# A two-layer transformer on one core: pieces of the next projection issued in front of the turns of the softmax weights

## Chip, cores and metric

One core of a Trainium2 chip runs the whole program. The metric is device time in microseconds (us) from one launch: before the change the median of three runs is 591.26 us (590.09 to 594.53).

The engines are called by the profile's names: PE (matrix multiplies), PEld (the loading of their weights), DVE (vector engine), ACT (activation engine), POOL (GpSimd), SP (the queue that issues most DMAs). Each engine takes its own instructions in the order in which the program issues them; between engines only semaphores order the work.

## Reference

Two layers over x of 8 x 256 tokens x 128 channels. Each layer normalises x and adds an attention and a mixture of experts, both computed from the normalised x. Only layer 1 is touched here:

```python
# layer 1, xn = layernorm(x): 8 heads of queries, one head of keys and values, causal
q = (xn @ Wq + bq) + pe          # 8 heads x 128
k, v = split(xn @ Wkv + bkv);  k = k + pe
probs = softmax(mask(q @ k.T / sqrt(128)))
attn = (probs @ v) @ Wo
# 8 experts, each token takes the one of its largest gate
h = gelu(xn @ w1[e] + b1[e]);  ffn = (h @ w2[e] + b2[e]) * score
x = x + attn + ffn
```

## The kernel before

All arithmetic is in f32. The 2048 tokens are 16 tiles of 128, four blocks of 512 and eight batches of 256. Layer 0 fills the first 335 us of the span; layer 1 is one loop over the batches b = 0 to 7 (L1458 to L1493) and a short end for the last batch.

**A batch.** Its scores come in three parts u[0], u[1], u[2] of 128 query rows x 1024 columns: u[0] is the first 128 queries against 128 keys for all 8 heads, u[1] and u[2] the second 128 queries against 256 keys for four heads each. For each part:

- `l1_scores` (L1275): 8 multiplies (16 instructions for u[0], 4 heads and 8 instructions for the others) on PE into one of two large PSUM tiles;
- `l1_maxima` (L1289): DVE adds the causal mask (L1291) and takes row maxima (L1295);
- `l1_exp` (L1297): ACT takes one exponential per head (L1301), which frees the large PSUM tile;
- `l1_weigh` (L1309): DVE takes reciprocals of the sums (L1311), then POOL scales the weights (L1313; DVE does it for three parts of batches 6 and 7);
- `l1_turn` (L1321): DVE transposes the weights in 32 x 32 blocks (L1328), "the turn".

The product of weights and values (`l1_pv`, L1336, 72 multiplies) of batch b is issued in batch b+1 by `l1_previous` (L1446), after the scores of u[0] and u[1] of b+1; ACT copies its result out of PSUM (L1358). `l1_finish` (L1360) multiplies it with Wo and adds the result to the accumulator on DVE (L1373). PE issues the scores of u[2] after the product of values, since they need the PSUM tile of u[0].

**The projections of the next block.** Queries and keys of a block serve two batches. `l1_project` (L799) is a generator of 9 pieces for a block: the keys and eight heads of queries. A piece is one 128x512 multiply on PE (L807, two instructions) into one of three PSUM banks and one DVE instruction that adds bias and positions and writes SBUF (L814). Batches 0, 2 and 4 start a new block and issue 2 + 3 of its pieces, batches 1, 3 and 5 issue the other 2 + 2 (L1480 and L1489). Batches 6 and 7 have none left.

**Filling work.** `fill(b, k)` (L1416) issues what a table assigns to three places in the batch: in batches 0 to 2 the router (L1152, L364), in batches 3 to 5 the experts (`l1_experts`, L1242), in batches 5 to 7 the gathers of the experts' rows (`l1_back`, L1391). An expert tile is a multiply "up" (L1210, 8 instructions), a Gelu on ACT (L1219) and a multiply "down" (L1228, 8 instructions) with a DVE addition (L1237); every fourth tile needs four transposes on PE (L1200) and a copy on DVE (L1202). ACT loads another table when it goes from exponentials to Gelu and back. All of these, the pieces of the projections and `l1_finish` take turns on the same three PSUM banks ("bank", L105), so an instruction on PE may wait until DVE or ACT has read an earlier bank.

**The order around the change** is written out by hand (L1474 to L1493): on DVE the maxima of u[2], the turn of u[0], then the filling work of place 0, two pieces, and the reciprocals of u[1]; later the addition of `l1_finish`, the turn of u[1], two or three pieces, the turn of u[2], and the filling work of place 2.

Of the kernel before, what the change touches and what calls it, by code (L numbers as in the profile page):

```python
# [62 lines left out]
def two_layer_kernel(  # L63
# [48 lines left out]
    def seq(ins):  # L112

        return tc.keep_in_program_order(ins)
# [684 lines left out]
    def l1_project(blk):  # L799

        qT = work.tile([P, H1, BLK], F32, tag="qk", name=f"qT1_{blk}")
        kT = work.tile([P, BLK], F32, tag="kT1", name=f"kT1_{blk}")
        qk1[blk] = (qT, kT)
        for h in range(-1, H1):
            pos = (pe_s if h < 0 else peq_s).unsqueeze(1).to_broadcast([P, 2, S])
            ps = bank(f"qk1_{blk}_{h}")
            seq(nc.tensor.matmul(  # L807
                ps,
                lhsT=wk1_s if h < 0 else wq1_s[:, h, :],
                rhs=xT[:, ts(blk, BLK)],  # L810
                start=True,
                stop=True,
            ))
            seq(nc.vector.scalar_tensor_tensor(  # L814
                (kT if h < 0 else qT[:, h, :]).rearrange("p (b s) -> p b s", b=2),
                ps.rearrange("p (b s) -> p b s", b=2),
                bk1_s if h < 0 else bq1_s[:, h : h + 1],
                pos,
                ALU.add,
                ALU.add,  # L820
            ))
            yield

    project1 = l1_project(0)
# [299 lines left out]
    def l0_end(first, second):  # L1124

        l1_scores(first)
        l1_maxima(first)
        l0_drain(*last0)
        l1_scores(second)
        l0_finish(B - 1, l0_turn_back(*done))  # L1130
        norm1[NBLK - 1].moments()
        l1_maxima(second)
# [142 lines left out]
    def l1_scores(u):  # L1275
        qT, kT = qk1[u.b // 2]
        o = (u.b % 2) * S
        u.ps = big_tile(f"s_{u.name}")
        u.sc = u.ps.rearrange("p (h k) -> p h k", h=u.nh)
        for h in range(u.nh):  # L1280
            seq(nc.tensor.matmul(  # L1281
                u.sc[:, h, :],
                lhsT=qT[:, u.h0 + h, ds(o + u.t * P, P)],
                rhs=kT[:, ds(o, u.nk)],
                start=True,
                stop=True,
            ))

    def l1_maxima(u):  # L1289
        diag = u.sc[:, :, ds(u.t * P, P)]  # L1290
        seq(nc.vector.tensor_tensor(  # L1291
            diag, diag, mask.unsqueeze(1).to_broadcast([P, u.nh, P]), ALU.add
        ))
        u.m = small.tile([P, H1], F32, tag="m1", name=f"m1_{u.name}")
        seq(nc.vector.tensor_reduce(u.m[:, : u.nh], u.sc, AX.X, ALU.max, negate=True))  # L1295

    def l1_exp(u):  # L1297
        u.p = work.tile([P, u.nh, u.nk], F32, tag="e", name=f"p_{u.name}", bufs=4)
        u.sums = small.tile([P, H1], F32, tag="sums1", name=f"sums1_{u.name}")
        for h in range(u.nh):  # L1300
            seq(nc.scalar.activation(  # L1301
                u.p[:, h, :],
                u.sc[:, h, :],
                AF.Exp,
                bias=u.m[:, h : h + 1],
                accum_out=u.sums[:, h : h + 1],
            ))

    def l1_weigh(u):  # L1309
        rec = small.tile([P, H1], F32, tag="rec1", name=f"rec1_{u.name}")  # L1310
        seq(nc.vector.reciprocal(rec[:, : u.nh], u.sums[:, : u.nh]))  # L1311
        engine = nc.vector if (u.b, u.t, u.h0) in ON_VECTOR else nc.gpsimd
        seq(engine.tensor_tensor(  # L1313
            u.p, u.p, rec[:, : u.nh].unsqueeze(2).to_broadcast([P, u.nh, u.nk]), ALU.mult
        ))
# [5 lines left out]
    def l1_turn(u):  # L1321


        if u.h0 == 0:
            turned[u.b, u.t] = work.tile(
                [P, H1, u.nk], F32, tag="c" if u.t else "h", name=f"pT_{u.name}"
            )
        seq(nc.vector.transpose(  # L1328
            turned[u.b, u.t][:, ds(u.h0, u.nh), :].rearrange("p h k -> p (h k)"),
            u.p.rearrange("p h k -> p (h k)"),  # L1330
        ))
# [28 lines left out]
    def l1_finish(b, tt, oT):  # L1360
        ps = (bank if b + 1 < B else big_tile)(f"wo1_{b}_{tt[0]}")
        for t in tt:
            for h in range(H1):
                seq(nc.tensor.matmul(  # L1364
                    ps[:, ts(t, P)],
                    lhsT=oT[:, h, ts(t, P)],
                    rhs=wo1_s[:, h, :],
                    start=(h == 0),
                    stop=(h == H1 - 1),
                ))  # L1370
        n, c = 2 * b + tt[0], ds(tt[0] * P, len(tt) * P)
        a = acc[:, ds(n, len(tt)), :].rearrange("p t c -> p (t c)")
        seq(nc.vector.tensor_tensor(a, ps[:, c], a, ALU.add))  # L1373
        if b >= 6:
            nc.sync.dma_start(out_t[:, ds(n, len(tt)), :], acc[:, ds(n, len(tt)), :])
# [40 lines left out]
    def fill(b, k):  # L1416
        for f, args in between1.get((b, k), ()):
            f(*args)
# [27 lines left out]
    def l1_previous(b):  # L1446

        nonlocal oT
        if b > 0:
            po = l1_banks(b - 1)  # L1450
            for t in range(2):
                l1_pv(b - 1, t, po)
            if b + 1 < B:
                l1_spread(b + 1)
            oT = work.tile([P, H1, S], F32, tag="c", name=f"oT_{b - 1}")
            l1_out(slice(None), po, oT)

    for b in range(B):  # L1458
        u = [Part(b, k) for k in range(len(PARTS))]
        if b % 2 == 0 and b + 2 < B:  # L1460
            project1 = l1_project(b // 2 + 1)
        if b == 0:
            l0_end(u[0], u[1])
        else:
            l1_scores(u[0])
            l1_maxima(u[0])
            l1_scores(u[1])
            l1_maxima(u[1])
        l1_exp(u[0])
        l1_previous(b)  # L1470
        if b == 0:
            fill(b, 0)
        l1_weigh(u[0])
        l1_scores(u[2])  # L1474
        l1_maxima(u[2])
        l1_exp(u[1])
        l1_turn(u[0])
        if b > 0:
            fill(b, 0)
        for _ in range(2):  # L1480
            next(project1, None)
        l1_weigh(u[1])
        l1_exp(u[2])
        fill(b, 1)
        l1_weigh(u[2])
        if b > 0:
            l1_finish(b - 1, (0, 1), oT)
        l1_turn(u[1])
        for _ in range(3 - b % 2):  # L1489
            next(project1, None)  # L1490
        if b + 1 < B:
            l1_turn(u[2])
            fill(b, 2)  # L1493
# [100 lines left out]
```

## Time and profile before

| | |
|---|---|
| median of three runs | 591.26 us |
| the profiled execution's own time | 584.82 us |
| span of the profiled execution | 583.0 us |
| busy, share of the span | PE 85%, PEld 61%, DVE 62%, ACT 42%, POOL 35% |
| mean granted PE clock | 0.938 |
| the 24 turns, L1328 | 29.5 us, 1232 ns each; DVE idle ahead of them 7.1 us |
| 24 of the 27 pieces' DVE part in this loop (queries), L814 | 17.0 us, 733 ns each |

A batch begins here with the first mask addition on DVE (L1291 of u[0]), by the timeline:

| batch | 0 | 1 | 2 | 3 | 4 | 5 | 6 | 7 |
|---|---|---|---|---|---|---|---|---|
| start, us | 335.98 | 362.27 | 386.83 | 414.42 | 459.75 | 498.88 | 529.04 | 550.53 |

In a timeline a line is one or more instructions of a kind: start, duration, engine, line, operation, output and inputs, and in brackets how long the engine sat idle before and which instruction released it. In a table by windows the columns are the stretch, its length, busy time and number of instructions of PE, PEld, DVE, ACT and POOL, the granted PE clock as a share of full speed, the DMA share and GB/s.

### The profile page before, as it was taken

The page shows a single profiled execution, that of the slowest core. Times are in us where ns is not written, and L with a number is a line of the kernel's source. Part 1 is how long each engine was busy: PE and PEld are TensorE (multiplying, and loading weights), DVE is VectorE, ACT ScalarE, POOL GpSimd, SP SyncE. Part 2 cuts the span into 40 slices and gives each one's busy share as a digit, 9 for nine tenths or more (in the row PEclk, how much of TensorE's full clock was granted, in tenths as well). Part 3 has the DMA queues.
Part 4 walks back from the last instruction along what each step waited for, and adds up shares of the span by engine and source line. Part 5 has one row for each costly group of instructions (what it writes and reads, how often), then busy time and mean ns, then how long its engine had stood idle before and what let it go on. Part 6 is the DMA issues. An engine that isn't in the chain of part 4 may idle for free.

```text
span 583.0 us, 11267 instructions
## 1 busy us (share of the span) xinstructions
PE 497.3 (85%) x3996; PEld 354.1 (61%) x3996; DVE 359.4 (62%) x733; ACT 246.6 (42%) x681; POOL 205.6 (35%) x254
## 2 busy tenths in 40 slices
PE   4887688889998899967899968877969989989777
PEld 1633345656766577543554736666667878978666
DVE  5487954646756467637797467787633544527662
ACT  4616123434443254313443551523255584665161
POOL 6230023266432440274372032212576041124740
PEclk9999786989999799989999997996989999999977
DMA  3600411324443231011021130171048465512111
GB/s 108 189 1 19 133 33 44 110 72 121 126 128 105 74 77 38 28 46 29 17 69 45 37 92 19 37 200 41 25 108 234 145 149 180 158 55 64 33 32 56
DMA packets 61925, 47.78 MB, mean 82 GB/s; under 512 B 6389, under 2 KB 56781, under 8 KB 61869
## 3 DMA queue, kind: packets, MB, share of 16 engines
q1 hardware_dynamic: 57453, 38.59, 23.3%
q0 software_dynamic: 3840, 8.26, 5.9%
q8 instruction: 32, 0.52, 0.4%
q10 hardware_dynamic: 576, 0.20, 0.1%
q14 instruction: 24, 0.20, 0.1%
HBM read 38.78 MB, written 8.26 MB: 81 GB/s over the span
## 4 chain that ended last, share of the span: by engine, by line
PE 56%; DVE 20%; issue 9%; ACT 6%; POOL 4%; DMA 1%; SPq 0%; another core or an unknown queue 0%; POOLq 0%; ACTq 0%; DVEq 0%
PE s L894 7%; PE u L692 6%; PE pv L967 5%; PE s L1281 4%; PE d L709 4%; DVE mx L909 4%; PE u L1210 3%; PE o L1345 3%; PE d L1228 3%; PE qk L807 3%; PE s L940 3%; PE wo L1364 3%; ACT p L1301 2%; PE ds L760 2%; PE sh L745 2%
## 5 line engine op out<-in xcount | busy, mean ns | idle before, releaser
L952 ACT ACTIVATE eT<-s 128x1024 f32<-128x1024 f32 x64 | 65.5, 1024 | 138.9 <-PE s L940 95.7
L909 DVE TENSOR_REDUCE mx<-s 128x4 f32<-128x1024 f32 x64 | 77.7, 1220 | 32.0 <-PE s L940 14.3
L513 POOL DMA_INDIRECT xs<-xd,idx x62 | 63.0, 1016 | 67.0 <-issue 57.8
L894 PE MATMUL s<-qk 32*128 32x256 f32 x512 | 74.4, 422 | 13.6 <-DVE mx L909 8.8
L1313 POOL TENSOR_TENSOR p<-p,rec 128x1024 f32<-128x1024 f32 x21 | 39.8, 1896 | 112.3 <-DVE rec L1311 112.2
L1301 ACT ACTIVATE p<-s,m 128x256 f32<-128x256 f32 (+1 forms) x128 | 52.5, 443 | 62.5 <-DVE m L1295 51.0
L940 PE MATMUL s<-qa,qk 32*128 32x256 f32 x512 | 75.6, 414 | 2.5 <-DVE qa L921 2.3
L894 PEld LDWEIGHTS s<-qk 32*128 32x128 f32 x512 | 43.2, 195 | 41.7 <-DVE mx L909 17.9
L513 POOL DMA_INDIRECT yt<-yg,idx x48 | 48.9, 1020 | 47.1 <-issue 37.2
L1281 PE MATMUL s<-kT,qT 128*128 128x128 f32 (+1 forms) x256 | 49.8, 348 | 9.1 <-ACT p L1301 4.3
L940 PEld LDWEIGHTS s<-qa,qk 32*128 32x128 f32 x512 | 45.9, 192 | 10.6 <-DVE qa L921 5.0
L1345 PE MATMUL o<-pT,vrep 32*128 32x256 f32 x576 | 48.9, 407 | 3.9 <-DVE pT L1328 2.2
L1281 PEld LDWEIGHTS s<-kT,qT 128*128 128x128 f32 x256 | 40.0, 200 | 18.2 <-issue 6.9
L1345 PEld LDWEIGHTS o<-pT,vrep 32*128 32x128 f32 x576 | 40.5, 197 | 11.6 <-DVE pT L1328 2.4
L692 PE MATMUL u<-xg,gu_s 128*88 128x128 f32 x312 | 42.6, 278 | 1.6 <-issue 1.6
L967 PE MATMUL pv<-eT,va 128*32 128x256 f32 x512 | 39.3, 412 | 1.5 <-issue 1.4
L692 PEld LDWEIGHTS u<-xg,gu_s 128*88 128x88 f32 x312 | 37.1, 160 | 3.8 <-issue 3.8
L1219 ACT ACTIVATE h<-u,own_b 128x128 f32<-128x128 f32 x92 | 25.9, 375 | 27.7 <-PE u L1210 25.2
L1291 DVE TENSOR_TENSOR s<-s,mask 128x512 f32<-128x512 f32 (+1 forms) x24 | 20.9, 869 | 25.2 <-PE s L1281 21.5
L1364 PE MATMUL wo<-wo_s,oT 128*128 128x128 f32 x256 | 34.0, 297 | 2.1 <-DVE qT L814 1.8
L1364 PEld LDWEIGHTS wo<-wo_s,oT 128*128 128x128 f32 x256 | 33.0, 212 | 3.9 <-issue 3.3
L1328 DVE STREAM_TRANSPOSE pT<-p 128x1024 f32<-128x1024 f32 x24 | 29.5, 1232 | 7.1 <-POOL p L1313 7.1
(222 smaller groups left out, 843.2 us busy)
## 6 DMA issues: line engine op xcount, KB each, us to landing
w_up<-in_w_dram SPq DMA_DIRECT2D x30, 256.0 KB
gu_s<-in_gu_dram SPq DMA_DIRECT2D x39, 176.0 KB
vrep<-vd SPq DMA_DIRECT2D x32, 128.0 KB
w_down<-in_w_dram SPq DMA_DIRECT2D x16, 256.0 KB
yg<-ys SPq DMA_DIRECT2D x14, 256.0 KB
dn_s<-in_dn_dram SPq DMA_DIRECT2D x39, 88.0 KB
bias<-in_b_dram SPq DMA_DIRECT2D x23, 64.0 KB
acc<-in_x_dram SPq DMA_DIRECT2D x4, 256.0 KB
```

The source lines that it names most:

```text
L513: seq(nc.gpsimd.indirect_dma_start(out=dst, out_offset=None, in_=table, in_offset=bass.IndirectOffsetOnAxis(ap=idx[:, k : k + 1], axis=0), ...
L692: seq(nc.tensor.matmul(ps[:IC, ts(c, P)], lhsT=gu0_s[:, i % RING0, c, :], rhs=xg0.get(i), start=True, stop=True,))
L894: seq(nc.tensor.matmul(pv[:, jj, t, :], lhsT=qT[r : r + ROW, g, ds(o + t * P, P)], rhs=kT[r : r + ROW, g, ds(o, S)], start=True, stop=True,))
L909: seq(nc.vector.tensor_reduce(m[:, ds(2 * half, 2), :, D0 * ((g + 1) % NG)], pv, AX.X, ALU.max, negate=True))
L940: seq(nc.tensor.matmul(pv[:, jj, c, :], lhsT=kT[r : r + ROW, g, ds(o + c * P, P)], rhs=qa[r : r + ROW, g, :], start=True, stop=True,))
L952: seq(nc.scalar.activation(eT.rearrange("p j c q -> p (j c q)"), ps, AF.Exp, scale=SC0))
L967: seq(nc.tensor.matmul(po[ds(ROW * j, ROW), ts(g % 2, S)], lhsT=va_flat[:, ds(o, ROW)], rhs=eTs[j // 2][:, j % 2, c, :], start=(c == 0), s ...
L1281: seq(nc.tensor.matmul(u.sc[:, h, :], lhsT=qT[:, u.h0 + h, ds(o + u.t * P, P)], rhs=kT[:, ds(o, u.nk)], start=True, stop=True,))
L1301: seq(nc.scalar.activation(u.p[:, h, :], u.sc[:, h, :], AF.Exp, bias=u.m[:, h : h + 1], accum_out=u.sums[:, h : h + 1],))
L1313: seq(engine.tensor_tensor(u.p, u.p, rec[:, : u.nh].unsqueeze(2).to_broadcast([P, u.nh, u.nk]), ALU.mult))
L1345: seq(nc.tensor.matmul(po[n][:, ts(t, H1 * ROW)], lhsT=vrep[r : r + ROW, b % 2, j, :], rhs=pT[r : r + ROW, :, j, :], start=(j == 0), stop= ...
L1364: seq(nc.tensor.matmul(ps[:, ts(t, P)], lhsT=oT[:, h, ts(t, P)], rhs=wo1_s[:, h, :], start=(h == 0), stop=(h == H1 - 1),))
```

## The change

The change touches only the order of issue in the loop over batches. Up to batch 5 the two pieces come in front of the turn of u[0] instead of behind it, and the two or three later pieces come in front of the turn of u[1]. In batches 1 to 7 the filling work of place 0 also comes in front of the turn of u[0], and behind the two pieces. No instruction is added or removed. On PE the only new order is that in batches 1 to 5 two pieces precede the filling work of place 0; on ACT, POOL and SP every queue keeps its order.

```diff
@@ -1474,20 +1474,20 @@
         l1_scores(u[2])
         l1_maxima(u[2])
         l1_exp(u[1])
-        l1_turn(u[0])
+        for _ in range(2):
+            next(project1, None)
         if b > 0:
             fill(b, 0)
-        for _ in range(2):
-            next(project1, None)
+        l1_turn(u[0])
         l1_weigh(u[1])
         l1_exp(u[2])
         fill(b, 1)
         l1_weigh(u[2])
         if b > 0:
             l1_finish(b - 1, (0, 1), oT)
-        l1_turn(u[1])
         for _ in range(3 - b % 2):
             next(project1, None)
+        l1_turn(u[1])
         if b + 1 < B:
             l1_turn(u[2])
             fill(b, 2)
```

## Prediction

> **What bounds the kernel now.** I read the busy shares, the chain of work that ended last, what waits for the pieces' DVE part, then the timeline of each engine, batch by batch, and last the clock in stretches of 2 us. No engine bounds the loop throughout. Batches 0 to 2 are paced by DVE (router work, maxima, turns), batches 3 to 5 by PE and ACT in turn (experts), 6 and 7 by the softmax chain and the gathers. So each edit is worth only what its own batch lets through.
>
> Who waited for L814 from batch 0 on:
>
> ```profile
> who waited for it (us, times):
>   PE vg L784: 4.9, 1
>   PE wo L1364: 2.1, 2
>   PEld s L1281: 1.6, 2
>   PEld qk L807: 1.4, 1
>   PE s L1281: 1.3, 2
> ```
>
> A piece late on DVE holds a PSUM bank or a head of queries, so PE waits. The list adds up to some 11 us, but PE and its weight loads are counted side by side, and not all of it is on the path. The change lets these DVE parts run before a 1.2 us turn. The turns themselves can hardly gain (7.1 us of idle ahead of them, 2.95 of it in batch 0, the rest in batches 6 and 7, which have no pieces).
>
> DVE in batch 0:
>
> ```profile
> 349.31 1.25 DVE L1328 STREAM_TRANSPOSE pT<-p 128x1024 f32<-128x1024 f32 x1 [2.95 <-POOL p L1313]
> 350.48 0.71 DVE L814 SCALAR_TENSOR_TENSOR kT<-qk_-1_3850,bk_s,pe_s 128x512 f32<-128x512 f32 x1
> ```
>
> DVE is idle for 2.95 us, waiting for POOL, with a ready piece (PE was done with it at 344.4) behind the turn.
>
> DVE, PE in batch 3:
>
> ```profile
> 425.76 1.23 DVE L1328 STREAM_TRANSPOSE pT<-p 128x1024 f32<-128x1024 f32 x1
> 426.92 0.65 DVE L1202 COPY xgT<-xgT 128x512 f32<-128x512 f32 x1
> ```
> ```profile
> 423.69 0.60 PE L1200 MATMUL xgT<-ident,xs 128*128 128x128 f32 x4
> 427.68 2.72 PE L1210 MATMUL u<-xgT,w_up 128*128 128x128 f32 x15 [3.38 <-issue]
> ```
>
> PE stands still for 3.38 us, until DVE has done mask, maxima, turn and copy. What follows that gap is dear, as the windows show (clock in the third column from the end):
>
> ```profile
> 390.00:392.00 2.00, 0.00 (x0) 0.00 (x0) 1.18 (x1) 2.00 (x13) 0.00 (x0) 0.76 1.03 313
> 392.00:394.00 2.00, 1.61 (x4) 1.34 (x5) 0.20 (x1) 2.00 (x6) 1.29 (x1) 0.50 0.84 255
> ...
> 426.00:428.00 2.00, 0.33 (x3) 0.35 (x4) 1.57 (x2) 0.63 (x1) 1.69 (x3) 1.00 0.27 64
> 428.00:430.00 2.00, 2.00 (x15) 2.00 (x14) 0.00 (x0) 1.06 (x4) 1.42 (x3) 0.64 0.14 41
> 430.00:432.00 2.00, 2.00 (x11) 2.00 (x11) 0.00 (x0) 1.23 (x5) 1.70 (x2) 0.50 0.67 191
> ```
>
> After a gap the clock falls to half and stays there until a whole stretch of some 3.4 us is busy. From these fractions the falls lie at 350.1, 391.0, 401.3 and 428.6, the rises at 356.9, 397.8, 408.0 and 432.0: all whole multiples of 3.41 us apart.
>
> **The change, part by part** (times on the span of 583.0; a minus is earlier).
>
> *Batch 0, +0.1.* The two DVE parts go into the 2.95 us gap (2 x 0.7). The values' multiply (L784, at 351.33, idle 4.87 for this piece) then waits only for ACT's copy of the turned x, which ends at 350.2: 1.0 earlier. But its three following pieces run at half clock, 1.7 us each (PE 353.28 on), and now stand ahead of the turn of u[1]: DVE takes them at about 354.0, 355.9 and 356.8, then two turns (2.3), and ends at 359.8 instead of 359.7. Ends: -1.4 with the clock up, +1.1 if the multiply doesn't start earlier.
>
> *Batch 1, +1.2.* DVE is busy without a break from 369.86 to 391 and does the same work in another order: 0. The cover for the pieces is that PE finishes them (370.1 to 372) while DVE does the maxima. What is new is a gap: the product of values starts 1.1 earlier (it follows batch 0's last pieces and scores on PE), but the scores of u[2] still wait for ACT at 367.8. PE's idle 1.1 us there becomes 2.2. The nearest row is 390 to 392: after 2.4 us of product of values and 1.0 of idle within one 3.41 us stretch, the clock fell. Price: u[2]'s scores take 3.78 instead of 1.99 (both rows of L1281, at 392.39 and 367.83), +1.8, and the two pieces follow at half clock, together +2.7. Ends 0 and +2.7; I take +1.2, somewhat under half.
>
> *Batch 2, 0 for DVE, -1.0 for PE.* The order of DVE's 10 us changes, not the sum. At its end three pieces run 408.7 to 412.3; the third waits for the bank of the first, held by the turn (PE at 411.17, 1.4 us PEld wait). With the pieces first PE goes on at 410.1, and batch 3's scores come 1.1 earlier. The turns of u[1], u[2] end at 414.2 as before. Batch 3's product of values and u[2]'s scores run end to end on PE and keep 1.0.
>
> *Batch 3, -4.4 in all.* Place 0: u[2]'s maxima end at 424.7; two DVE parts (1.3) stand where one turn (1.16) stood, the copy is done at 426.7, and "up" starts at 426.8 instead of 427.68: -0.9. PE meanwhile does the two pieces (1.7), so the gap of 3.38 shrinks to about 1.8. A gap of 1.76 at 372.0 left the clock at 1.0. At full clock the 24 "up" take 2.7 instead of 4.55 and the first 8 "down" 0.9 instead of 1.7. Then the next four transposes must wait for rows that POOL gathers until 427.9 (landing about 430, estimated from the 2.06 us of an expert result's landing). The fourth tile's "up" starts about 431.4 instead of 435.15: -3.7. That two pieces (1.72) no longer stand at 437.04 brings nothing more: from there ACT paces (Gelu, table 1.28, four exponentials, table 1.28, Gelu of the next tiles at 442.17), and keeps -3.7. After `l1_finish` a piece no longer waits for the turn of u[1], and "down" at 453.19, idle 0.63 for that bank, starts 0.7 earlier. Sum -4.4. Ends: without the clock -1.6, with rows landing early -5.0.
>
> *Batch 4, -0.9.* The pieces leave 476.50 to 478.22 and fill a PE wait of 1.84 at 470.98 (for ACT's Gelu). ACT again paces after its table loads, until the Gelus at 481.57; from there the last "up" (483.27, behind a "down" idle 0.78) can come 0.9 earlier, and the output multiply with it. Ends -1.7 (all kept) and +0.15 (ACT keeps all).
>
> *Batch 5, 0.* The same move, into a wait of 1.39, but the batch ends on ACT: table, exponentials, table, Gelu at 519.81, "down" idle 0.93 for it. Ends -0.3, +0.35. Behind it the turn of u[1] and the pieces change places with the same sum before 529.04.
>
> *Batches 6 and 7, 0.* No pieces; the filling work of place 0 is two gathers on POOL with no DVE part. The turn of u[0] now also passes the expert additions of batches 3 to 5; the reciprocals of u[1] queue behind it. That costs nothing: POOL weighs u[1] at 440 to 442, its turn comes at 451. Without this cover it would be 1.2 per batch. POOL, SP and ACT keep their order; their gathers and weight loads only start earlier.
>
> **Sum:** 0.1 + 1.2 - 4.4 - 0.9 = -4.0. On the profiled execution: 584.8 - 4.0 = 580.8, of which 1.8 lies outside the span. The median of the runs is 6.4 above that execution, so the same difference gives 591.3 - 4.0 = 587.3.
>
> **A rule against the rows.** The Trainium skill, "TensorE: Matmul & The Clock Gate", "What's actually happening": the clock halves after a whole idle window of about 3.4 us, and that window runs freely, so its position differs between runs. The period agrees with the 3.41 us above. The length does not: the gap from 389.97 to 392.39 was 2.42 and the clock fell. By the rule, batch 1's gap of 2.2 costs nothing, and the sum is -5.2; by the row, -4.0. The second half speaks against me: batch 3's gain from the clock exists only in runs whose window falls into the old gap. With neither clock term the sum is 0.1 - 1.6 - 0.9 = -2.4. The rows decide for me: four of the four gaps between 2.4 and 4.9 us in batches 0 to 3 brought a fall, though in one execution.
>
> **Rivals.**
>
> *Absorbed.* The pieces move, the clock in batch 3 stays as it was (it falls after the shorter gap too, or had not fallen in most runs). For it: one execution's window position. Against: the gap halves. -2.4, or 0 if ACT also keeps batch 4's share: 589 to 591.
>
> *Larger.* Batch 0's shorter wait (4.87 to 3.9) leaves the clock up there, and batch 1's gap is harmless. -1.4 - 5.0 - 1.7 = -8.1: 583.2. Against: 3.9 us idle is still longer than the gaps that brought a fall.
>
> *Slower: turns queued behind half-speed pieces.* In batches 0 to 2 the path is DVE, and a piece ahead of a turn makes DVE wait for PE: at half clock a piece takes PE 1.7 and DVE 0.7, so each costs 1.0. Batch 0: +1.1; batch 1: +2.7 and +2.0 for the second pair, if the clock stays down through the output multiply; batch 2, 3 pieces: +3.0, less 0.6 of idle that is there now: 8.2 together. It decides once it exceeds batch 3 to 5's 5.3 by the whole: from six half-speed pieces on the path. 591.3 + 2.9 = 594.2. Against: at 408.7 the clock was back at 1.0 for the three pieces of batch 2.
>
> **How the numbers follow.** My case 0.47 (583.5 to 590 by its own ends), absorbed 0.22, larger 0.14, slower 0.17. A difference under 1% (5.9 us) is about what a measurement of this kernel can't tell from none. Faster by over 1% (below 585.3): most of the larger case and a quarter of mine, 0.25. Slower by over 1% (above 597.2) takes all of the half-speed pieces and a batch 3 without its clock gain (594.2 + 2.8 = 597.0): somewhat over half of the slower case, 0.10. Within: 0.65. Range 583.0 to 594.0.
>
> **What would show it.** Right: L784 starts within 4 us of the transposes before it; PE's gap ahead of the first L1210 is below 2 us with clock 1.0 over the following 4 us; no piece after L1228 at the middle of batch 4; the batches' first masks come at about 362.4, 388.1, 415.7, 456.6, 494.9 and 525.0 (batches 1 to 6). Wrong: clock 0.5 at 428 in spite of the short gap; idle of DVE before L814 growing from 2.9 us to over 6; turns waited for by L1345. A change at 529 that is not in the end would be the clock in batch 7's two falls, which is chance.

## The result, and the profile after

The changed kernel takes 592.86 us (median of 20 runs), the kernel before 587.94 us (20 runs, the three of the start among them): 1.0088 times as long, 95% interval 1.006 to 1.0116. It is about 5 us slower, where I forecast 4 us faster. The median of the kernel before is by now 3.3 us below the 591.26 of three runs from which I counted.

The page of the changed kernel begins with the span; its row of PE gives the busy us of each engine:

```profile
span 587.1 us, 11268 instructions
...
PE 493.4 (84%) x3996; PEld 351.1 (60%) x3996; DVE 359.2 (61%) x733; ACT 246.9 (42%) x681; POOL 205.7 (35%) x254
```

The work is the same (PE is busy 3.9 us less, at a mean clock of 0.945 for 0.938), yet the span is 4.1 us longer. Time was lost in waits. The batches, by the first mask addition as before:

| batch | 0 | 1 | 2 | 3 | 4 | 5 | 6 | 7 |
|---|---|---|---|---|---|---|---|---|
| length before, us | 26.29 | 24.56 | 27.59 | 45.33 | 39.13 | 30.16 | 21.49 | 32.47 |
| length after, us | 26.56 | 24.55 | 27.19 | 45.36 | 40.87 | 32.95 | 23.00 | 30.78 |
| difference | +0.27 | -0.01 | -0.40 | +0.03 | +1.74 | +2.79 | +1.51 | -1.69 |
| forecast | +0.1 | +1.2 | 0 | -4.4 | -0.9 | 0 | 0 | 0 |

The differences add up to +4.24; layer 0 ended 0.14 earlier. The -1.0 that I forecast for PE in batch 2 stands in no column: my sum left it out, without a reason. Who waits for L814 from batch 0 on:

```profile
who waited for it (us, times):
  PEld u L1210: 2.0, 1
  PE u L1210: 1.8, 1
...
```

The two entries that I had aimed at, L784 with 4.9 and L1364 with 2.1, are gone (L784) or down to 0.6 (L1364, in a line left out here). That part of the reasoning held. DVE in batch 0:

```profile
346.12 0.74 DVE L814 SCALAR_TENSOR_TENSOR kT<-qk_-1_3848,bk_s,pe_s 128x512 f32<-128x512 f32 x1
...
349.16 1.25 DVE L1328 STREAM_TRANSPOSE pT<-p 128x1024 f32<-128x1024 f32 x1 [1.63 <-POOL p L1313]
...
357.53 2.36 DVE L1328 STREAM_TRANSPOSE pT<-p 128x1024 f32<-128x1024 f32 x2
```

The pieces now lie in DVE's old gap, whose rest is 1.63 us. The two later turns follow the later pieces, and end at 359.9; the prediction had 359.8. Batch 3, on PE, on DVE and on ACT:

```profile
426.08 2.94 PE L1210 MATMUL u<-xgT,w_up 128*128 128x128 f32 x24 [1.77 <-DVE qT L814]
...
435.03 2.08 PE L1210 MATMUL u<-xgT,w_down 128*128 128x128 f32 x8 [2.82 <-DVE xgT L1202]
```
```profile
425.34 0.68 DVE L1202 COPY xgT<-xgT 128x512 f32<-128x512 f32 x1
434.28 0.69 DVE L1202 COPY xgT<-xgT 128x512 f32<-128x512 f32 x1 [8.26 <-remote]
```
```profile
434.14 1.14 ACT L1219 ACTIVATE h<-u,own_b 128x128 f32<-128x128 f32 x4 [3.15 <-remote]
```

The gap ahead of the first "up" is 1.77 for 3.38, and the 24 "up" run in 2.94 at full clock. But the second copy comes at 434.28, before it came at 434.40, and so "up" of the fourth tile starts at 435.03 for 435.15. The last line is the Gelu of the third "up": it too comes only at 434.14, though the profile's modelled end of all 24 products is 429.02. So DVE and ACT see PE's results 3.6 and 5.1 us behind their modelled ends here. The windows show the clock (third column from the end):

```profile
428.00:430.00 2.00, 1.35 (x13) 1.11 (x11) 0.00 (x0) 0.57 (x3) 1.59 (x2) 1.00 0.70 188
...
434.00:436.00 2.00, 0.97 (x4) 0.97 (x5) 0.89 (x2) 1.14 (x4) 1.01 (x1) 0.66 0.21 52
436.00:438.00 2.00, 2.00 (x12) 2.00 (x11) 0.00 (x0) 0.80 (x4) 1.39 (x3) 0.50 0.68 187
```

It stays up at 428, and falls at 434 instead, in the new wait for the copy. What PE gained it only waited out later. Leaving aside batches 6 and 7, whose differences nearly cancel, the loss lies in batches 4 and 5. PE in batch 5 before, then after:

```profile
514.74 1.88 PE L807 MATMUL qk<-xT,wq_s 128*128 128x512 f32 x4
...
520.23 1.26 PE L1228 MATMUL d<-w_up,h 128*128 128x128 f32 x8 [0.93 <-ACT h L1219]
521.33 3.74 PE L1364 MATMUL wo<-wo_s,oT 128*128 128x128 f32 x32
```
```profile
509.22 1.88 PE L807 MATMUL qk<-xT,wq_s 128*128 128x512 f32 x4
...
522.15 1.26 PE L1228 MATMUL d<-w_up,h 128*128 128x128 f32 x8 [2.65 <-ACT h L1219]
523.25 5.36 PE L1364 MATMUL wo<-wo_s,oT 128*128 128x128 f32 x32
```

In the batch's own time the last "down" starts at 21.35 before and at 21.78 after, only 0.43 later. The pieces (1.9 us) no longer stand in the middle, so PE waits 2.65 there for 0.93. The clock falls behind that gap (0.50 from 524 to 526), and the output multiply takes 5.36 for 3.74. The third loss, 0.73, is the hand-over to batch 6: two turns follow the two last pieces (the pieces had run on PE while DVE did a turn), and this cover is gone.

### The profile page after: what moved, and what is told of

Read it like the earlier page. It is cut to its first block, busy times and chain, and to the rows that moved or that the text cites. A ratio compares the mean times of both kernels' runs of the same rounds, so it can differ in the third digit from the quotient of the medians.

```text
span 587.1 us, 11268 instructions
## 1 busy us (share of the span) xinstructions
PE 493.4 (84%) x3996; PEld 351.1 (60%) x3996; DVE 359.2 (61%) x733; ACT 246.9 (42%) x681; POOL 205.7 (35%) x254
## 3 DMA queue, kind: packets, MB, share of 16 engines
q0 software_dynamic: 3840, 8.26, 6.0%
HBM read 38.78 MB, written 8.26 MB: 80 GB/s over the span
## 4 chain that ended last, share of the span: by engine, by line
PE 50%; issue 15%; DVE 15%; ACT 6%; DMA 3%; POOL 3%; another core or an unknown queue 3%; SPq 1%; POOLq 0%; ACTq 0%; DVEq 0%
PE s L894 6%; PE u L692 6%; PE o L1345 6%; PE s L1281 5%; PE d L709 4%; PE pv L967 4%; PE s L940 3%; PE qk L807 3%; ACT p L1301 3%; DVE mx L909 2%; PE d L1228 2%; PE sh L745 2%; PE u L1210 2%; DVE m L1295 2%
## 5 line engine op out<-in xcount | busy, mean ns | idle before, releaser
L894 PEld LDWEIGHTS s<-qk 32*128 32x128 f32 x512 | 41.9, 189 | 39.2 <-DVE mx L909 16.4
L1345 PEld LDWEIGHTS o<-pT,vrep 32*128 32x128 f32 x576 | 41.4, 205 | 11.4 <-DVE pT L1328 2.4
L967 PE MATMUL pv<-eT,va 128*32 128x256 f32 x512 | 37.5, 397 | 1.6 <-issue 1.5
L807 PE MATMUL qk<-xT,wq_s 128*128 128x512 f32 x64 | 33.5, 635 | 2.4 <-DVE acc L1373 2.4
L677 DVE SCALAR_TENSOR_TENSOR sg<-sg,u 88x256 f32<-88x256 f32 x39 | 16.2, 416 | 30.6 <-ACT sg L676 22.3
L1364 PE MATMUL wo<-wo_s,oT 128*128 128x128 f32 x256 | 32.1, 286 | 2.7 <-ACT oT L1358 2.1
```

Source lines behind the costliest of these rows:

```text
L807: seq(nc.tensor.matmul(ps, lhsT=wk1_s if h < 0 else wq1_s[:, h, :], rhs=xT[:, ts(blk, BLK)], start=True, stop=True,))
L894: seq(nc.tensor.matmul(pv[:, jj, t, :], lhsT=qT[r : r + ROW, g, ds(o + t * P, P)], rhs=kT[r : r + ROW, g, ds(o, S)], start=True, stop=True,))
L967: seq(nc.tensor.matmul(po[ds(ROW * j, ROW), ts(g % 2, S)], lhsT=va_flat[:, ds(o, ROW)], rhs=eTs[j // 2][:, j % 2, c, :], start=(c == 0), s ...
L1345: seq(nc.tensor.matmul(po[n][:, ts(t, H1 * ROW)], lhsT=vrep[r : r + ROW, b % 2, j, :], rhs=pT[r : r + ROW, :, j, :], start=(j == 0), stop= ...
```

## The experiments

The change has two moves. The first is made around the turn of u[0] and has two halves: on DVE the turn goes behind the fill and the pieces, on PE the pieces go ahead of the fill. The second puts the later pieces ahead of the turn of u[1]. I write P for the two pieces, F for `fill(b, 0)`, T for the turn of u[0]: before is T F P, after is P F T. The runs were made in three sets, each with runs of the kernel before among them. That kernel took 583.21, 548.57 and 547.80 us in the three sets. In the traces the difference between the sets lies in layer 0 (its end at 331 to 337 us in the first set, at 303 to 306 in the others) and in batch 3 (45.3 us and more, against 39.6 to 41.4). In batch 3 of all six profiles of the first set (those before and after the change among them) ACT or DVE starts 1.7 to 6.0 us behind the modelled end of the product that it needs; in the eight others the copy ahead of the fourth "up" and the Gelu behind it come within 0.1 us. Why is open; it is not the chip, which was the same in the first two sets. The changed kernel itself was measured in the runs of the result alone. Ratios are to the same set.

**First set: the moves apart.** e1, P F T with the second place as before:

```diff
-        l1_turn(u[0])
+        for _ in range(2):
+            next(project1, None)
         if b > 0:
             fill(b, 0)
-        for _ in range(2):
-            next(project1, None)
+        l1_turn(u[0])
```

> Only the first move (two pieces and the filling work of place 0 in front of the turn of u[0]); the later pieces stay behind the turn of u[1]. Theory A (PE order): two pieces ahead of the expert work put the first 'up' 1.7 us later, ACT's table load waits for it, and 'down' and the weight loads behind it on SP come late: this carries the loss, +2 to +4.5 us of the whole change's +5; batch 4 about +1.7 longer than the 39.1 us of before, table load idle on PE about 1.1 us in batches 4 and 5. Theory B (DVE order: turns queue behind pieces that PE paces): only the part of the first turn, +0 to +1. Theory C (the clock's falls by chance): within 1 us of before.

e2, the second move alone:

```diff
-        l1_turn(u[1])
         for _ in range(3 - b % 2):
             next(project1, None)
+        l1_turn(u[1])
```

> Only the second move (two or three pieces in front of the turn of u[1]). Theory A: +0.5 to +1.5 us, from the end of batch 5 alone, where the first mask of batch 6 comes 0.7 later after the output addition (4.67 us behind it in the changed kernel, 3.94 before). Theory B: +3 to +5 us. Theory C: within 1 us of before.

e3, PE's half of the first move alone, T P F:

```diff
         l1_turn(u[0])
+        for _ in range(2):
+            next(project1, None)
         if b > 0:
             fill(b, 0)
-        for _ in range(2):
-            next(project1, None)
```

> The turn of u[0] first, then the two pieces, then the filling work of place 0: the order of PE as in the changed kernel, the turn as before; the later pieces as before. Theory A: +2 to +4.5 us, as with the whole first move. Theory B: 0 to +0.5. Theory C: within 1 us of before.

e4, DVE's half alone, F P T:

```diff
-        l1_turn(u[0])
         if b > 0:
             fill(b, 0)
         for _ in range(2):
             next(project1, None)
+        l1_turn(u[0])
```

> The filling work of place 0, then the two pieces, then the turn of u[0]: the order of PE as before, only the turn goes last on DVE; the later pieces as before. Theory A: -1 to +0.5 us (the copy ahead of the first 'up' no longer waits for the turn). Theory B: +1 to +2. Theory C: within 1 us of before.

Measured: e1 584.45 us, 1.0037 [1.0009, 1.0065]; e2 590.77 us, 1.015 [1.0093, 1.0207], from 6 runs only; e3 587.46 us, 1.0074 [1.0039, 1.0108]; e4 580.49 us, 0.9973 [0.9944, 1.0001]. The two halves of the first move have opposite signs: PE's order costs, DVE's order gains if anything. That speaks for theory A. e2 fits no number of any theory and was repeated (in its profile batch 3 takes 48.23, with a PE wait of 4.69 for nothing that the profile shows).

**Second set: which batches.** e5 is e2 again; e6 makes the second move in batches 0 to 3 only.

> The second move alone, in every batch, a second time: the first time it gave 1.015 [1.0093, 1.0207] from few runs, more than the whole change (1.0088). Theory A (the cost lies in TensorE's order of the first move; the second move costs only the lost cover in batches of three pieces, +0.7 us in batch 5's hand-over): 583.7 to 584.7 us against 583.2, ratio 1.001 to 1.003. Theory B (the turns of u[1] queue behind pieces that wait for TensorE, and the next exponentials come late in several batches): +3 us or more, ratio above 1.005. Theory C (only chance falls of the clock): ratio within 0.998 to 1.002.

```diff
-        l1_turn(u[1])
-        for _ in range(3 - b % 2):
-            next(project1, None)
+        if b < 4:
+            for _ in range(3 - b % 2):
+                next(project1, None)
+            l1_turn(u[1])
+        else:
+            l1_turn(u[1])
+            for _ in range(3 - b % 2):
+                next(project1, None)
```

> The second move alone, in batches 0 to 3 only; batches 4 and 5 keep the order of before. If the cost of the second move is the lost cover at the end of batch 5 (three pieces of which none is hidden; theory A), nothing of it is left: ratio 0.998 to 1.001, perhaps -0.7 us from batch 3, where the product down no longer waits for a piece. If it is the turns queued behind pieces (theory B), it lies in batches 0 to 3 as well, and two thirds of whatever the second move costs in all remain: ratio above 1.004.

Measured: e5 550.93 us, 1.0037 [1.0008, 1.0067]; e6 546.86 us, 1.0009 [0.9973, 1.0044]. So 1.015 did not come again, and the second move costs about 0.4% (2 us) when made alone. That is somewhat more than A's 0.1 to 0.3%. e5's batch 5 is 0.72 longer than e6's (30.89 and 30.17), the lost cover, as A had it.

e7 has P F T in batches 0 to 3 and F P T in 4 and 5, e8 has P F T in 4 and 5 and the order of before elsewhere (both leave the second place as before):

```diff
-        l1_turn(u[0])
-        if b > 0:
-            fill(b, 0)
-        for _ in range(2):
-            next(project1, None)
+        if b < 4:
+            for _ in range(2):
+                next(project1, None)
+            if b > 0:
+                fill(b, 0)
+            l1_turn(u[0])
+        else:
+            if b > 0:
+                fill(b, 0)
+            for _ in range(2):
+                next(project1, None)
+            l1_turn(u[0])
```

> The first move with the turn of u[0] last, but TensorE keeps the order of before (fill ahead of pieces) in batches 4 and 5; pieces ahead of fill in batches 0 to 3. Theory A: batch 4 is back at 38.3 to 39.1 us (from 40.9 to 42.5) and batch 5 at 29.2 to 30.9 (from 30.6 to 33.0), batch 3 stays at 45.4 where fill first gave 45.3 to 51.1; time 579 to 581.5 us against 583.2, ratio 0.993 to 0.997. Theory C: as before within 0.2%.

> The complement: the first move complete (pieces, fill, turn of u[0]) in batches 4 and 5 only. Theory A: batch 4 takes some 41 us for 39.1 and batch 5 some 31.5 for 30.2, since the load of ACT's table waits for a product up that stands behind the pieces, and SP's loads of weights follow the product down: +2.7 and +1.7 us, 587.6 us against 583.2, ratio 1.004 to 1.0085. Theory C: ratio within 0.998 to 1.002.

Measured: e7 541.06 us, 0.9884 [0.9846, 0.9921]; e8 552.56 us, 1.007 [1.0031, 1.011]. The price of PE's order lies in batches 4 and 5, and the first move without it is faster than the kernel before, by more than the 0.3 to 0.7% that A gave it. To see why, take batch 4 with the order of before (e6, whose batches 4 and 5 are unchanged), PE and then SP's queue:

```profile
443.95 1.06 PE L1210 MATMUL u<-xgT,w_down 128*128 128x128 f32 x8
```
```profile
434.96 0.41 SPq L1184 DMA_DIRECT2D w_down<-in_w_dram  x1
...
437.51 0.34 SPq L1183 DMA_DIRECT2D w_down<-in_w_dram  x1
```

and with the pieces first (e8), in the same order:

```profile
446.11 1.44 PE L1210 MATMUL u<-xgT,w_down 128*128 128x128 f32 x8 [2.59 <-DMA w_down<-in_w_dram]
...
451.65 2.08 PE L1210 MATMUL u<-xgT,w_up 128*128 128x128 f32 x8 [0.38 <-DVE ys L1237]
```
```profile
438.19 0.41 SPq L1184 DMA_DIRECT2D w_down<-in_w_dram  x1
...
439.74 0.34 SPq L1183 DMA_DIRECT2D w_down<-in_w_dram  x1
```

Batch 4 starts at 423.70 in e6 and at 424.63 in e8. The first "down" stands 2.2 us later in e8 (at 12.37 of the batch for 10.17), and with it the load that reuses its weights, L1184 at 13.56 for 11.26. The next load of "up" weights, L1183, goes out at 15.11 for 13.81, and the "up" that uses them starts at 21.48 for 20.25: 6.4 us behind its load in both. In e8 this load sets the time. In e6 two pieces stand on PE in the middle of the batch, between the load and that "up", and PE waits for nothing. In e8 they have already been spent, and PE waits 2.59. Behind this wait the clock falls (0.50 from 448 to 452): the next "up" takes 2.08, where at full clock it takes 1.06. Of the 4.5 us that batch 4 loses (43.65 for 39.13), 1.2 are the later "up" and 3.3 follow it, at half clock for the most part. The length of the wait and the fall differ between the profiles with the pieces first: 0.72 without a fall in e3 (41.25), 1.34 without one after the change (40.87), 1.76 with one in e1 (42.45), 2.67 with one in e9 (43.74).

**Third set: the table load, and the parts again.** In e8, as after, ACT's table load ahead of the first Gelu also comes late: it waits 1.13 us for the first "up", where in e6 it waits for nothing. This was my first explanation (theory A). e9 is e8 with a Gelu of one column put ahead of the pieces, so that the table is loaded early (it is issued in batches 6 and 7 too, which have no pieces):

```diff
+        if b >= 4:
+            warm = small.tile([P, 1], F32, tag="warm", name=f"warm_{b}", bufs=1)
+            seq(nc.scalar.activation(warm, own_b1[:, 0, 0:1], AF.Gelu))
```

> The first move complete in batches 4 and 5 only, as in e8, and ahead of the pieces ScalarE gets one Gelu of 128x1 that waits for nothing, so that its table is loaded at 10.6 us of the stage and not behind the first product up at 11.7. Theory A as first put (the late table load is what costs): 1.1 us of each of the two batches come back, ratio 1.002 to 1.004 where e8 gave 1.007. Theory A2, from the traces of e6 and e8 (batch 4 loses because the pieces no longer cover the load of expert weights, which SyncE issues 2.3 us later, behind the first product down; batch 5 loses 0.43 us of TensorE's own order and 1.6 us of clock after a gap of 2.65 us): the table load comes 1.1 us earlier and nothing follows from it, ratio 1.005 to 1.009.

Measured: 550.86 us, 1.0079 [1.0053, 1.0104]. ACT in batch 4 of e9 (start at 422.53):

```profile
433.10 1.28 ACT L1479 ACT_TABLE_LOAD   x1
...
434.50 1.12 ACT L1219 ACTIVATE h<-u,own_b 128x128 f32<-128x128 f32 x4
```

and PE:

```profile
444.10 1.47 PE L1210 MATMUL u<-xgT,w_down 128*128 128x128 f32 x8 [2.67 <-DMA w_down<-in_w_dram]
```

The Gelu starts at 11.97 of the batch for 12.99 in e8, a full 1.0 us earlier, and nothing follows from it: PE waits for the same weights until 21.57, batches 4 and 5 take 43.74 and 32.20 for 43.65 and 32.22. Theory A as first put has fallen; the version with the weights' load (A2) holds, with the clock behind the wait in batch 4 as well, which it had named in batch 5 alone.

e10 puts only T last in batches 4 and 5 (F P T), all else as before:

```diff
+        if b < 4:
             l1_turn(u[0])
             if b > 0:
                 fill(b, 0)
             for _ in range(2):
                 next(project1, None)
+        else:
+            if b > 0:
+                fill(b, 0)
+            for _ in range(2):
+                next(project1, None)
+            l1_turn(u[0])
```

> In batches 4 and 5 only the turn of u[0] is put behind fill and pieces, whose order stays fill, pieces; all else as before. Theory A2: the copy of the gathered tokens no longer stands behind the turn on VectorE (1.24 us), so the wait of 1.84 us in batch 4 and of 1.39 in batch 5 goes: -1.4 and -0.9 us, ratio 0.995 to 0.997. If all of the gain of e7 (0.9884) came from there, 0.9884; if it came from batches 0 to 3 alone, 1.000.

Measured: 544.88 us, 0.9969 [0.9947, 0.9991]. ACT, DVE and PE in batch 4 of e6 (the order of before, start at 423.70):

```profile
435.58 1.14 ACT L1219 ACTIVATE h<-u,own_b 128x128 f32<-128x128 f32 x4
```
```profile
435.78 0.65 DVE L1202 COPY xgT<-xgT 128x512 f32<-128x512 f32 x1
```
```profile
436.77 1.16 PE L1210 MATMUL u<-xgT,w_up 128*128 128x128 f32 x8 [1.84 <-ACT h L1219]
```

and DVE and PE in e10 (start at 424.69):

```profile
435.61 0.68 DVE L1202 COPY xgT<-xgT 128x512 f32<-128x512 f32 x1
```
```profile
436.35 1.16 PE L1210 MATMUL u<-xgT,w_up 128*128 128x128 f32 x8 [0.43 <-DVE xgT L1202]
```

The second "up" waits 0.43 where before it waited 1.84. In e6 it starts 0.05 behind the end of the Gelu (436.72) and 0.34 behind that of the copy (436.43), so the wait was for the Gelu, as the profile says. In e10 it starts 0.06 behind the end of the copy and before the Gelu of the tile ahead of it has begun (436.56). The copy holds the rows of later tiles; what can tie this product to the copy or to the Gelu is the PSUM bank that either has to read first. Moving the turn, which touches no bank, has changed for which of the two the product waits: it seems to have got another of the three banks, though no trace names the bank. Batch 4 takes 37.72 for 39.13 and batch 5 29.24 for 30.17: 2.3 us, 0.4%, with PE's order untouched; e7, e11 and e12 repeat these two lengths to 0.05, except batch 5 of e11, which has the second move (29.97).

e11 is the whole change, both moves, with F P T in batches 4 and 5; e12 is e7 again.

> The whole change, both moves, but in batches 4 and 5 fill stands ahead of the pieces on TensorE again and the turn of u[0] is last. Theory A or A2: the price of pieces ahead of fill (e8, +0.7%) goes and the gain of the turn behind fill (-0.4%) comes, so the change's 1.0088 falls to 0.997 to 1.000; the second move's part (e5, +0.4%) stays. If the second move is what costs, as its first measurement (1.015) had it: 1.005 or more.

> The kernel of e7 once more, unchanged: the first move with the turn of u[0] last, pieces ahead of fill in batches 0 to 3, fill ahead of pieces in batches 4 and 5, the second place as before. If e7's gain is the order's and not that of its day: ratio within 0.985 to 0.993. If it was an outlier: above 0.994.

Measured: e11 544.13 us, 0.9954 [0.993, 0.9978]; e12 540.73 us, 0.9859 [0.9796, 0.9921]. With one order changed in two batches the slower kernel has become a faster one, and by more than the 0 to 0.3% that was expected of e11. e7's gain came again, and e12 (6 runs) differs from e11 only in the second move. DVE in batch 0 of e11:

```profile
320.72 0.75 DVE L814 SCALAR_TENSOR_TENSOR qT<-qk,bq_s,peq_s 128x512 f32<-128x512 f32 x1 [0.53 <-PE qk L807]
322.43 0.75 DVE L814 SCALAR_TENSOR_TENSOR qT<-qk,bq_s,peq_s 128x512 f32<-128x512 f32 x1 [0.96 <-PE qk L807]
323.59 0.75 DVE L814 SCALAR_TENSOR_TENSOR qT<-qk,bq_s,peq_s 128x512 f32<-128x512 f32 x1 [0.41 <-PE qk L807]
```

and of e12:

```profile
321.13 1.21 DVE L1328 STREAM_TRANSPOSE pT<-p 128x1024 f32<-128x1024 f32 x1
322.27 2.25 DVE L814 SCALAR_TENSOR_TENSOR qT<-qk,bq_s,peq_s 128x512 f32<-128x512 f32 x3
```

The clock is at half in both. In e11 DVE waits 1.90 us for three pieces and only then does two turns; in e12 a turn fills that wait. Batch 0 takes 26.57 and 24.61. Lengths by order, from the profiles of the second and third sets:

| order (u[0] place, u[1] place) | 0 | 1 | 2 | 3 | 4 | 5 |
|---|---|---|---|---|---|---|
| before's (e10 in 0-3, e6 in 4, 5) | 26.30 | 24.55 | 27.61 | 39.75 | 39.13 | 30.17 |
| both moves (e11 in 0-3) | 26.57 | 24.55 | 27.19 | 39.59 | | |
| first move alone (e12 in 0-3, e8 in 4, 5) | 24.61 | 24.55 | 25.22 | 39.78 | 43.65 | 32.22 |
| turn of u[0] last (e12 in 4, 5) | | | | | 37.72 | 29.24 |

The first move alone gains 1.7 us in batch 0 and 2.4 in batch 2; the second gives back 2.0 in each. In batch 2 it is the clock. The scores of u[2] at the batch's start, PE in e11 and then in e12:

```profile
359.23 2.50 PE L1281 MATMUL s<-kT,qT 128*128 128x256 f32 x5 [3.53 <-ACT p L1301]
```
```profile
358.28 1.99 PE L1281 MATMUL s<-kT,qT 128*128 128x256 f32 x8 [2.41 <-ACT p L1301]
```

With the second move PE has finished the product of values earlier and waits 3.53 for ACT, at half clock afterwards (5 of the 8 products take 2.50). Over all profiles: the gap was 3.53 in five (after, e2, e5, e6, e11), and the clock fell in all five; 2.41 in seven, and it fell in five (before, e4, e8, e9, e10) and not in two (e3, e12); 0.8 in two (e1, e7), where it did not fall there. With 2.41, then, it is chance, and batch 2's 2.4 us in this table is the difference between a run of e12 without that fall and one of e10 with it; with 3.53 the fall came each time.

## Why the prediction was wrong, point by point

*Batch 0, +0.1: right* (+0.27). The two effects that I set against each other are both real and measured apart: the first move brings -1.7 (e12 against e10), and three half-speed pieces ahead of a turn cost +2.0 (e11 against e12).

*Batch 1, +1.2: the gap was right, its price was spared by chance* (-0.01). The gap came as forecast, 2.23 for 1.10, and in this profile the clock stayed up. PE after the change, and in e5:

```profile
367.96 1.99 PE L1281 MATMUL s<-kT,qT 128*128 128x256 f32 x8 [2.23 <-ACT p L1301]
```
```profile
335.04 3.53 PE L1281 MATMUL s<-kT,qT 128*128 128x256 f32 x8 [2.23 <-ACT p L1301]
```

Seven profiles have a gap of 2.2 to 2.3 here. The clock fell in five of them (e1, e2, e4, e5, e6), where the batch takes 25.42 to 26.18 for 24.55, and not in two (after, e11). So the price is 0.9 to 1.6 when it comes, not 2.7, and it comes more often than I took. This and the wider gap in batch 2 are what the second move costs beside the lost cover.

*Batch 2, 0 on DVE and -1.0 on PE: right on PE, and left out of the sum.* The batch is 0.40 shorter. On PE the scores of u[2] start 5.58 us into batch 3 for 7.44.

*Batch 3, -4.4: failed* (+0.03). Its signs came true (gap 1.77, clock 1.0 at 428) and its conclusion did not. The step that failed is "the fourth tile's 'up' starts about 431.4 instead of 435.15". The copy ahead of it waited 8.26 us and came when it had come before. In the third set, without the late results of the first, the first "up" starts 12.52 us into the batch with the order of before (e10), 12.66 with the first move (e12) and 11.54 with both (e11), and the batch takes 39.75, 39.78 and 39.59: an "up" 1.0 earlier is worth 0.2, so it is hardly on the path to the batch's end. The clock I had too dear: e9 has the order of e10 here, and with its clock fallen (24 "up" in 4.29 for 2.92) the batch takes 41.00, 1.2 more. And the 0.9 from DVE's order rests on a slip: I let u[2]'s maxima end at 424.7, where they begin; they end at 425.84, as the start of the turn at 425.76 in my own lines could have told. Two pieces' parts (1.4) for one turn (1.2) then make the copy later, as the 0.14 between e10 and e12 shows. That the first "up" came 1.3 earlier in the batch all the same is the work of the second move, through batch 2's end: in e2, with that move alone, it starts at 11.40, where it started at 13.25. Only the 0.7 behind L1364 came: from acc to the next batch's mask 8.13 us for 8.82.

*Batch 4, -0.9: wrong sign* (+1.74). I let the pieces "fill a PE wait of 1.84 at 470.98 (for ACT's Gelu)" and costed the place they left, in the middle of the batch, at nothing. This step failed as well: the place was cover for the expert weights' load. After the change "up" waits 1.34 for that load; and the load itself is issued later, since on SP it follows a "down" that the pieces push back. I wrote that weight loads "only start earlier"; L1183 goes out at 15.34 of the batch for 13.81.

*Batch 5, 0: wrong* (+2.79). My bound of +0.35 for the order itself was near: 0.43. What I left out was that the pieces also kept a later gap short. It grew from 0.93 to 2.65, and the clock fell in three (after, e8, e9) of the five profiles with that gap, in none with 0.93; where it didn't fall (e1) the batch takes 30.58, 0.42 above before. In this profile the output multiply lost 1.62 to it. The rest is the 0.73 of the lost cover, which I had called the "same sum": the sum of DVE's work is the same, its wait for PE is not.

*Batches 6 and 7* (+1.51, -1.69) are falls of the clock at other moments. In batch 6 it fell behind a gap of 0.90 ahead of the scores; e11, with the same gap, has no fall there and takes 21.48, as before does.

*The rule on the clock.* I weighed the Trainium skill, "TensorE: Matmul & The Clock Gate", "What's actually happening" (a whole idle window of about 3.4 us is needed) against one row. Neither decides: gaps of 3.53 brought a fall in five of five, those of 2.2 to 2.3 in batch 1 in five of seven, those of 2.41 and 2.65 in eight of twelve. Falls also followed shorter ones: 0.90 (batch 6 after the change), 1.76 (batch 4 of e1), 1.84 (batch 4 of e5). So a whole idle window is not needed here, and none of these lengths was safe by itself; the 1.76 that I took for harmless was one case. I counted this risk at the gaps that I saw, and did not ask which gaps the move would open elsewhere.

*Rivals.* "Slower: turns queued behind half-speed pieces" has its mechanism (2.0 in batch 0) but not its size; what made the kernel slower was in batches 4 and 5, where none of my rivals looked.

Adding the parts by profile: first move in batches 4 and 5 with its clock falls as in the changed kernel's profile 1.74 + 2.06, the lost cover 0.73, batches 0 to 3 -0.1, together 4.4 us, against 5 measured (3.5 to 6.8 by the interval). These are parts of one profile of each kernel, so the sum is no test of the cause. The runs give one: e11 with the price of the pieces first in batches 4 and 5 (e8 against e10) is 0.9954 x 1.0070 / 0.9969 = 1.0055, against 1.0088 [1.006, 1.0116] for the whole change. The remaining 0.3% is no more than the intervals of the four ratios leave open.

What stays open is why the second copy in batch 3 does not come earlier in the first set: DVE waits for it 3.6 us beyond the modelled end of its transposes (430.68), as ACT waits for the third "up" before it, while in the third set (e12) the wait is 3.5 and ends with the transposes. So it is PE's results that come late, and not the copy alone; what holds them is not shown.

## What to carry to other kernels

Work that stands between two dependent steps may be the cover for a load or a table switch behind it: before moving it ahead, ask what PE will wait for at the place it leaves, and which queue issues its loads only after the steps that are now pushed back. An edit that reorders two engines' queues at once should be costed, and tried, as one edit for each: here, in two batches, the turn behind the fill was worth -0.3% (e10) and the pieces ahead of the fill cost 1.0% on top of it (e8 against e10), and the good part alone (e7, 0.9884) is faster than the kernel before. Moving an instruction on one engine can also change for what an instruction of another engine waits, where both share a ring of buffers: compare the releasers of the waits, and not only their lengths. And a wait costs more than its length when the clock falls behind it (here 1.2 us of wait and 3.3 behind it).

## What the runs showed of the hardware

The times of one kernel lie in groups that go with PE's clock: in the third set those of the kernel before lie mostly near 544.3, 546.6 and 548.6 us, with mean granted clocks of about 0.967, 0.960 and 0.947. In layer 1 the clock, where it was up, fell to half behind every gap on PE above 3 us (3.10 to 4.87, over all profiles), and behind some of the shorter ones, from 0.90 on. A table load of ACT waited for the operand of the activation behind it (1.13 us, until the first "up"), and an activation without an operand to wait for took the load out of that wait (e9, at 10.57 of the batch for 11.69).
